# A graph attention stage: units of two groups, one pacing wait each, parts of z added in PSUM

## The chip, the cores and the metric

The kernel runs on one core of a Trainium2 chip. The metric is the device time of one execution in microseconds, and the time of a kernel is the median of its runs. The engines are called PE (matrix products), DVE (vector), ACT (activations), POOL (here it issues the gathers) and SP (here it issues plain loads and stores).

## The reference

Three graph layers with means over neighbours, a layer norm, then one attention layer on the same graph, with a residual and a layer norm. Only the attention layer is touched by the change. N is 12500 nodes, E is 200000 edges (src, dst), D is 256, with K = 4 heads of R = 16.

```python
ZU = einsum('nd,kdr->knr', Z, U)              # 4 heads of 16 numbers for each node
zs = ZU[:, src, :]
zd = ZU[:, dst, :]
logits = (zs * zd).sum(-1) / sqrt(R)
alpha = softmax of logits over the edges of each dst
agg = segment_sum(alpha[..., None] * zs, dst)
ssa = einsum('k,knr,kdr->nd', softmax(head_w), agg, U)
Z_half = 0.5 * Z + 0.5 * ssa
grad_step = Z_half + 0.5 * ((Z_half - Z_half @ Dmat.T @ Dmat) @ Dmat)
x = layernorm(x + relu(grad_step - 0.05))
```

The edges are sorted by dst, so the edges of a node lie side by side.

## The kernel before, in words

The first 5560 us are the three graph layers, with which the change has nothing to do. Then `fast_attention` (from line 1006) works on the edges in **groups** of GT = 14 tiles of 128 edges, 112 groups, the last of 9 tiles. The nodes that the edges of one group meet fit in 128 rows from a start that is known for the group; `delta` holds how far the start moves from one group to the next. A row of `zu_d` holds the 64 numbers of a node (KR = 64).

For a group the kernel does the following.

- SP loads the rows of the group's own nodes (`zn`, the 64 numbers; `zb` and `zT`, the 256 numbers and their transpose) and, spread over all partitions, the position of each edge's dst among the group's rows (`ohT` before it is a one-hot).
- POOL issues 14 indirect gathers (`gather`, line 121), one for each tile, which fetch the row of each edge's source into `zs`.
- ACT makes the one-hot `ohT` (nodes by edges) in two instructions of 1792 elements, lines 1043 and 1044. DVE makes the other one-hot `oh` (edges by nodes), line 477.
- ACT and DVE split `zn` into a rounded part and the rest, the two parts of z, lines 1048 and 1049.
- **pD** (PE, line 1055): for each tile one matmul, ohT against both parts of z side by side, gives each edge the 64 numbers of its dst twice, 128 columns. Half a group of seven tiles fills 896 columns of PSUM.
- DVE multiplies this with `zs` (`zz`, line 1063, 896 elements) and sums it to the logits (`lg`, line 1066). ACT takes the exponential (line 1069) and copies it next to pD (line 1071), DVE multiplies with `zs` (`wf`, line 1072), and ACT and DVE split the result into two parts again (`w`, lines 1075 and 1076).
- **pA** (PE, line 1083): `oh` against `w`, added over the 14 tiles, gives for each node the sums over its edges. The edges of a node can begin in the group before, so `carry` (line 486) adds the previous group's sums, shifted by `delta`.
- ACT and DVE add the two parts (`part`, line 1091; `acc`, line 1093) and divide (`den`, `ag`, lines 415 to 418). PE turns the result (**pT**, line 1097), ACT copies it (`agT`, line 425), and PE makes the gradient step (**pO**, line 402 with `zT`, line 408 with `agT`).
- ACT and DVE finish: relu (line 432), residual, layer norm (lines 355 to 360), and SP stores 128 rows.

`group(g)` is a generator of five steps: gathers up to pD and `w`; pA with the carry; `part` up to pT; `agT` and pO; the end. `order_of` calls, for each new group, first the new group, then the next step of the four groups before it. `in_order` fixes the order of the matmuls on PE as they are written.

Two gathers of a group are held back. The first one (j = 0) waits for the last pD of the group before (`shown`), and the eighth (j = H) for the pA of two groups before (`summed`). In POOL's order, twelve free gathers of a group stand ahead of these held ones.

```python
if j == 0 and g:
    hold_back(shown[-1], i)
if j == H and 1 < g < NG - 1:
    hold_back(summed[g - 2], i)
```

Of the kernel before, what the change touches and what calls it, by code (L numbers as in the profile page):

```python
# [9 lines left out]
F32 = mybir.dt.float32  # L10
# [13 lines left out]
P = 128  # L24
NB = 125
TE = 125
GT = 14
# [21 lines left out]
def tile_gnn_resnorm(  # L49
# [70 lines left out]
    def gather(dst_ap, table, idx):  # L120
        return nc.gpsimd.indirect_dma_start(  # L121
            out=dst_ap, out_offset=None, in_=table,
            in_offset=bass.IndirectOffsetOnAxis(ap=idx, axis=0))
# [10 lines left out]
    def hold_back(first, then):  # L134

        tc.add_manual_dep(then.ins, first.ins.name, DONE, reason="the pace of the gathers")
# [317 lines left out]
    def load_rows(pairs, g, first_of=None):  # L454

        rows = group_rows(g, loads[0], AFTER, first_of)
        for t, table in pairs:
            loads[0] = nc.sync.dma_start(t, rows_of(table, rows))
# [15 lines left out]
    def onehot(wk, nodes, r, dt=F32, name="oh", op=OP.is_equal, bufs=2, m=GT, behind=None):  # L474

        oh = wk.tile([P, GT, P], dt, name=name, bufs=bufs)
        i = nc.vector.tensor_tensor(oh[:, :m], r[:, :m].unsqueeze(2).to_broadcast([P, m, P]),  # L477
                                    nodes.unsqueeze(1).to_broadcast([P, m, P]), op=op)
        if behind is not None:
            after(behind, i)  # L480
        return oh

    def carry(wk, pa, d, before):
        sh = wk.tile([P, P], F32, name="sh")
        nc.vector.tensor_scalar(sh, steps, d, None, op0=OP.is_equal)
        return nc.tensor.matmul(pa, sh, before, start=False, stop=True)  # L486

    def fast_sage():
        with ExitStack() as fx:
# [516 lines left out]
    def fast_attention():  # L1006
        loads[0] = None
        H = GT // 2
        with tc.tile_pool(name="att", bufs=2) as wk, \
                tc.tile_pool(name="att_c", bufs=1, space=PSUM) as cps, \  # L1010
                tc.tile_pool(name="att_ps", bufs=1, space=PSUM) as ps:
            nodes = group_consts(cps)
            order, sums = [None], [None]
            shown, summed = [], []

            def in_order(first, last):
                if order[0] is not None:
                    after(order[0], first)
                order[0] = last

            def group(g):

                T = GT if g < NG - 1 else LT
                zb = wk.tile([P, D], F32, name="zb", bufs=8)
                zT = wk.tile([P, DC, P], F32, name="zT", bufs=6)
                zn = wk.tile([P, KR], F32, name="zn", bufs=3)
                load_rows([(zn, zu_d), (zb, z_d), (zT, zt_d)], g)

                ohT = wk.tile([P, GT, P], F32R, name="ohT", bufs=3)
                rT = ohT.bitcast(F32)[:, :T].rearrange("p j e -> p (j e)")  # L1030
                nc.sync.dma_start(rT, rel_d[g * GT:g * GT + T, :].rearrange("j e -> (j e)")[None, :]
                                  .to_broadcast([P, T * P]))
                zs = wk.tile([P, GT, KR], F32, name="zs", bufs=6)
                for j in range(T):
                    i = gather(zs[:, j], zu_d, srcI[:, g, j:j + 1])

                    if j == 0 and g:
                        hold_back(shown[-1], i)
                    if j == H and 1 < g < NG - 1:
                        hold_back(summed[g - 2], i)  # L1040
                oh = onehot(wk, nodes, rel[:, g], F32R, bufs=3, m=T)
                oT = ohT[:, :T].rearrange("p j e -> p (j e)")
                nc.scalar.activation(oT, rT, AF.Abs, bias=npidx)
                nc.scalar.activation(oT, rT, AF.Relu, scale=-1.0, bias=1.0)

                z2 = wk.tile([P, K, 2, R], F32R, name="z2", bufs=3)
                zk = zn.rearrange("p (k r) -> p k r", r=R)
                nc.scalar.activation(z2[:, :, 0], zk, AF.Copy)
                nc.vector.tensor_tensor(z2[:, :, 1], zk, z2.bitcast(F32)[:, :, 0], op=OP.subtract)

                w = wk.tile([P, GT, 2 * AW], F32R, name="w", bufs=3)
                for a, n in ((0, H), (H, T - H)):

                    pd = ps.tile([P, (H + 1) * 2 * KR], F32, name="pD", bufs=2)
                    mm = [nc.tensor.matmul(pd[:, j * 2 * KR:(j + 1) * 2 * KR], ohT[:, a + j],  # L1055
                                           z2.rearrange("p k i r -> p (k i r)"), start=True, stop=True)
                          for j in range(n)]
                    in_order(mm[0], mm[-1])
                    shown.append(mm[-1])

                    zg = zs[:, a:a + n].rearrange("p t (k r) -> p (t k) r", r=R)
                    zz = wk.tile([P, H * K, 2, R], F32, name="zz")[:, :n * K]
                    nc.vector.tensor_mul(zz, zg.unsqueeze(2).to_broadcast([P, n * K, 2, R]),  # L1063
                                         pd[:, :n * 2 * KR].rearrange("p (m i r) -> p m i r", i=2, r=R))
                    lg = wk.tile([P, H, K], F32, name="lg")[:, :n]
                    nc.vector.reduce_sum(lg.rearrange("p t k -> p (t k)"), zz.rearrange("p m i r -> p m (i r)"),  # L1066
                                         axis=AX.X)
                    wf = wk.tile([P, H, AW], F32, name="wf")[:, :n]
                    nc.scalar.activation(wf[:, :, KR:], lg, AF.Exp, scale=0.25)
                    pe = pd[:, H * 2 * KR:H * 2 * KR + n * K].rearrange("p (t k) -> p t k", k=K)  # L1070
                    nc.scalar.activation(pe, wf[:, :, KR:], AF.Copy)
                    nc.vector.tensor_mul(wf[:, :, :KR].rearrange("p t (k r) -> p t k r", r=R),  # L1072
                                         zs[:, a:a + n].rearrange("p t (k r) -> p t k r", r=R),
                                         pe.unsqueeze(3).to_broadcast([P, n, K, R]))
                    nc.scalar.activation(w[:, a:a + n, :AW], wf, AF.Copy)
                    nc.vector.tensor_tensor(w[:, a:a + n, AW:], wf, w.bitcast(F32)[:, a:a + n, :AW], op=OP.subtract)
                yield
                own = None
                if g == NG - 1:
                    own, *mm = own_gradient(ps, zT)  # L1080
                    in_order(*mm)
                pa = ps.tile([P, 2 * AW], F32, name="pA")
                mm = [nc.tensor.matmul(pa, oh[:, j], w[:, j], start=j == 0, stop=g == 0 and j == T - 1)  # L1083
                      for j in range(T)]
                if g:
                    mm.append(carry(wk, pa[:, :AW], delta[:, g:g + 1], sums[0]))
                in_order(mm[0], mm[-1])
                summed.append(mm[-1])
                yield
                part = wk.tile([P, AW], F32, name="part")  # L1090
                nc.scalar.activation(part, pa[:, AW:2 * AW], AF.Copy)
                acc = wk.tile([P, AW], F32, name="acc", bufs=3)
                nc.vector.tensor_add(acc, part, pa[:, :AW])
                sums[0] = acc
                ag = attention_mean(wk, acc, 1e-30, OP.max)
                pt = ps.tile([P, P], F32, name="pT")
                mm = nc.tensor.transpose(pt[:KR], ag, ident)  # L1097
                in_order(mm, mm)
                yield
                agT = attention_turned(wk, pt, P)  # L1100
                pg, *mm = gradient_step(ps, zT, agT, own)
                in_order(*mm)
                yield
                o, made = attention_end(wk, zb, pg)
                store_rows([(o, out)], g, made)
                yield

            live = []  # L1110
            for g in range(NG):
                live.append(group(g))
                if g < NG - 1:
                    order_of = [g, *range(max(0, g - 4), g)]
                else:
                    order_of = [g, g - 4, g - 3, g - 2, g - 1, g - 3, g - 2, g - 1, g - 2, g - 1, g - 1] + [g] * 4
                for k in order_of:
                    next(live[k])
            assert all(next(s, 0) == 0 for s in live)


# [202 lines left out]
```

## Time and profile before

| what | value |
|---|---|
| runs | 7839.01, 7910.11, 7911.72 us, median 7910.11 |
| the profiled execution | 7864.61 us, span 7862.8 us |
| attention stage, first gather starts | 5562.54 us |
| attention stage, last gather starts | 7821.82 us |
| PE, DVE, ACT, POOL busy over the span | 70%, 48%, 43%, 61% |
| PE, DVE, ACT, POOL busy, 6000 to 7500 us | 48%, 52%, 44%, 66% |
| granted TensorE clock, whole span | 0.776 |
| granted TensorE clock, 6000 to 7500 us | 0.50 |
| one group, mean of 74 groups in 6000 to 7500 us | 20.27 us |

The profiled execution is one more execution, with its own time; sums over the trace are made against that time. A line of the groups of instructions gives the source line, the engine, the operation, the tile written and those read, the shape and the count, then the busy time and the mean duration in ns, and after the second bar the idle time of the engine just before these instructions, with what ended it. "Issue" is idle time in which nothing that the profile shows was waited for. A row of the timeline gives start, duration, engine, line and what was done, and in brackets how long the engine had been idle before it and what released it. PEld is PE's weight load. The ends of matmuls are modelled. Where the released instruction waited for several things, the profile names the one that came last by its records.

### The profile page before, as it was taken

To read this page: it belongs to the slowest core of one execution; us is meant where nothing else is said; L and a number is where in the kernel's file an instruction comes from. 1 tells how busy PE (TensorE), PEld (TensorE's weight loads), DVE (VectorE), ACT (ScalarE), POOL (GpSimd) and SP (SyncE) were. 2 spreads that over 40 slices of the span, in tenths; PEclk is the share of its full clock that TensorE was granted. 3 is DMA by queue.
4 is the path that set the end of the run, shared out by engine and by line. 5 is a ranking of instruction groups with operands and counts; after the bars stand their busy time and mean duration, and the time that the engine had idled before them with its cause. 6 is when DMAs were issued, how large, how long until landed. Compare 5 with 4: busy or idle time off the path is not lost.

```text
span 7862.8 us, 85871 instructions
## 1 busy us (share of the span) xinstructions
PE 5525.1 (70%) x23570; PEld 4415.0 (56%) x23570; DVE 3772.2 (48%) x9563; ACT 3353.2 (43%) x6092; POOL 4799.9 (61%) x4977
## 2 busy tenths in 40 slices
PE   4688888888588888888588888887444444444445
PEld 3466666666466666666476676665343443344344
DVE  4555444444244444344344555554455555555555
ACT  2333333333255555444354454444344444444443
POOL 5556656556466666565565565656466666666665
PEclk6899999889799999998798999998655555555555
DMA  7777777777466766665576676665222222222222
GB/s 209 243 235 233 247 235 249 235 238 249 154 218 215 225 217 221 202 217 184 161 220 200 212 225 209 213 195 168 89 92 91 88 89 91 91 85 92 91 87 67
DMA packets 896848, 1391.60 MB, mean 177 GB/s; under 512 B 191296, under 2 KB 540504, under 8 KB 892253
## 3 DMA queue, kind: packets, MB, share of 16 engines
q1 hardware_dynamic: 654927, 834.75, 32.3%
q0 software_dynamic: 213152, 496.65, 21.6%
q10 hardware_dynamic: 28270, 54.56, 2.0%
q8 instruction: 189, 3.10, 0.2%
q14 instruction: 310, 2.54, 0.1%
HBM read 1175.15 MB, written 210.33 MB: 176 GB/s over the span
## 4 chain that ended last, share of the span: by engine, by line
PE 27%; DVE 8%; issue 6%; another core or an unknown queue 4%; POOL 3%; DMA 3%; ACT 1%; DVEq 0%; ACTq 0%; POOLq 0%
PE px L783 8%; PE pD L1055 3%; PE pA L1083 3%; POOL zs L121 3%; PE pA L908 3%; DMA zs<-zu_d,srcI 3%; PE pO L402 2%; DVE zz L1063 2%; PE pO L408 2%; DVE lg L1066 1%; PE pO L375 1%; DVE wf L1072 1%; PE pT L384 1%; PE pA L486 1%
## 5 line engine op out<-in xcount | busy, mean ns | idle before, releaser
L121 POOL DMA_INDIRECT xg<-h_d,srcI x2128 | 2079.8, 977 | 1404.0 <-issue 646.9
L783 PE MATMUL px<-c,hz 128*128 128x512 f32 x8232 | 2396.7, 431 | 224.0 <-ACT c L777 106.1
L121 POOL DMA_INDIRECT zs<-zu_d,srcI x1563 | 1496.9, 958 | 821.5 <-issue 422.0
L783 PEld LDWEIGHTS px<-c,hz 128*128 128x128 f32 x8232 | 1593.9, 202 | 580.1 <-ACT c L777 126.8
L777 ACT ACTIVATE c<-c 128x1024 fp32r<-128x1024 uint8 (+1 forms) x1274 | 1119.1, 891 | 1431.1 <-remote 469.9
L121 POOL DMA_INDIRECT xg<-in_x_dram,srcI x1218 | 1159.9, 952 | 769.1 <-PE pA L911 304.5
L477 DVE TENSOR_TENSOR oh<-rel,gconst 128x1792 fp32r<-128x1792 f32 (+1 forms) x354 | 713.8, 2017 | 1239.2 <-PE pO L408 414.6
L902 DVE TENSOR_TENSOR hl<-xg,hl 128x256 fp32r<-128x256 f32 x2128 | 777.5, 419 | 509.2 <-ACT hl L900 370.1
L1097 PE MATMUL pT<-ident,ag 128*64 128x128 f32 x112 | 47.2, 422 | 1158.9 <-DVE ag L418 760.9
L900 ACT ACTIVATE hl<-xg 128x512 fp32r<-128x512 f32 x1216 | 619.9, 568 | 292.4 <-PE pA L908 62.1
L1097 PEld LDWEIGHTS pT<-ident,ag 128*64 128x64 f32 x112 | 14.4, 128 | 1238.4 <-DVE ag L418 813.1
L911 PE MATMUL pA<-xg,oh 128*128 128x258 f32 x2520 | 659.1, 418 | 58.7 <-ACT agg L933 36.9
L908 PE MATMUL pA<-hl,oh 128*128 128x512 f32 x2128 | 604.6, 421 | 85.3 <-issue 82.8
L911 PEld LDWEIGHTS pA<-xg,oh 128*128 128x128 f32 x2520 | 528.7, 212 | 166.1 <-ACT agg L933 42.2
L673 ACT ACTIVATE win<-pc 128x392 uint16<-128x392 f32 x512 | 252.5, 496 | 662.7 <-remote 222.9
L908 PEld LDWEIGHTS pA<-hl,oh 128*128 128x128 f32 x2128 | 419.6, 200 | 195.3 <-issue 96.9
L661 DVE TENSOR_SCALAR oa<-iota,kt 128x128 bf16<-128x128 f16 x1024 | 268.9, 263 | 278.2 <-PE pA L911 108.7
L1055 PE MATMUL pD<-z,ohT 128*128 128x128 f32 x1563 | 360.9, 418 | 54.2 <-DVE lg L1066 19.1
L365 DVE TENSOR_TENSOR pO<-b,pO 128x256 f32<-128x256 f32 x306 | 130.7, 427 | 533.2 <-remote 295.4
L1055 PEld LDWEIGHTS pD<-z,ohT 128*128 128x128 f32 x1563 | 346.9, 333 | 55.1 <-issue 25.3
L1063 DVE TENSOR_TENSOR zz<-zs,pD 128x896 f32<-128x896 f32 x224 | 242.1, 1081 | 272.5 <-DMA zs<-zu_d,srcI 137.9
L1083 PE MATMUL pA<-w,oh 128*128 128x136 f32 x1563 | 361.4, 418 | 0.0
(255 smaller groups left out, 7368.2 us busy)
## 6 DMA issues: line engine op xcount, KB each, us to landing
hz<-hs_d SPq DMA_DIRECT2D x637, 512.0 KB
c<-cnt_d SPq DMA_DIRECT2D x112, 896.0 KB
ohT<-rel_d SPq DMA_DIRECT2D x111, 896.0 KB
hs_d<-hs SPq DMA_DIRECT2D x218, 256.0 KB
cnt_d<-win ACTq DMA_DIRECT2D x32, 1568.0 KB
xg<-h_d,srcI POOLq DMA_INDIRECT x2128
c<-cnt_d SPq DMA_DIRECT2D x70, 448.0 KB
zs<-zu_d,srcI POOLq DMA_INDIRECT x1563
```

The lines of the kernel that those rows point to most:

```text
L121: return nc.gpsimd.indirect_dma_start(out=dst_ap, out_offset=None, in_=table, in_offset=bass.IndirectOffsetOnAxis(ap=idx, axis=0))
L477: i = nc.vector.tensor_tensor(oh[:, :m], r[:, :m].unsqueeze(2).to_broadcast([P, m, P]), nodes.unsqueeze(1).to_broadcast([P, m, P]), op=op)
L661: nc.vector.tensor_scalar(oa[:, c], iota16[:, :P], kt[:, 0, at], None, op0=OP.is_equal)
L777: nc.scalar.activation(c32.rearrange("p (k d) -> p k d", d=P), c8[:, :, b % CB], AF.Copy)
L783: made.append(nc.tensor.matmul(px[f][i], hz[:, b % ZB, a:a + P].bitcast(F32R), c32[:, i * 512:(i + 1) * 512], start=b == 0 and part == 0, ...
L900: nc.scalar.activation(hi[:, j:j + n, :W], xg[:, a + j:a + j + n, :W], AF.Copy)
L902: nc.vector.tensor_tensor(lo[:, j, :D], xg[:, a + j, :D], hf[:, j, :D], op=OP.subtract)
L908: mm.append(nc.tensor.matmul(pa, oh[:, a + j], hl[:, j].rearrange("p i d -> p (i d)"), start=first, stop=stop))
L911: mm.append(nc.tensor.matmul(pa[:, :W], oh[:, a + j], xg[:, a + j, :W], start=first, stop=stop))
L1055: mm = [nc.tensor.matmul(pd[:, j * 2 * KR:(j + 1) * 2 * KR], ohT[:, a + j], z2.rearrange("p k i r -> p (k i r)"), start=True, stop=True) f ...
L1063: nc.vector.tensor_mul(zz, zg.unsqueeze(2).to_broadcast([P, n * K, 2, R]), pd[:, :n * 2 * KR].rearrange("p (m i r) -> p m i r", i=2, r=R))
L1083: mm = [nc.tensor.matmul(pa, oh[:, j], w[:, j], start=j == 0, stop=g == 0 and j == T - 1) for j in range(T)]
```

## The change

The attention stage now works in units of two groups: `plan` has 54 pairs of groups and four single groups at the end.

- `unit(gs)` has one step for the loads, gathers and `ohT`; one for each half group of pD (four in a pair); one for each half group of `zz` to pA (four); then `acc` to pT, pO and the end, each done once for both groups. The calls are arranged so that, on PE, the pA halves of one unit alternate with the pD halves of the next.
- Of a unit's 28 gathers one is held back, the very first, by the last pD of the unit before. The wait for pA is gone.
- pD: for each tile two matmuls of 64 columns, one for each part of z, add in PSUM. A half group takes 448 columns, with the exponentials in the same bank. There are four such banks. `zz` and `lg` read 448 elements.
- A third one-hot, `past`, places the edges of the first group among the nodes of the second. The matmuls of the first group's halves are followed by seven more each, which add these edges to the second group's sums. The carry of the second group starts from the previous unit's sums, shifted by both steps (`two`).
- `zs` has three buffers of two groups, `zb` five, `zT` four, `w` six half groups, `oh` and `past` four in all.

The core of the diff:

```diff
-            def group(g):
+            def unit(gs):
...
-                    if j == 0 and g:
-                        hold_back(shown[-1], i)
-                    if j == H and 1 < g < NG - 1:
-                        hold_back(summed[g - 2], i)
+                        if i == 0 and j == 0 and shown:
+                            hold_back(shown[-1], it)
...
-                    mm = [nc.tensor.matmul(pd[:, j * 2 * KR:(j + 1) * 2 * KR], ohT[:, a + j],
-                                           z2.rearrange("p k i r -> p (k i r)"), start=True, stop=True)
-                          for j in range(n)]
+                    mm = [nc.tensor.matmul(pd[:, j * KR:(j + 1) * KR], ohT[:, i * GT + a + j], z2[:, i, part],
+                                           start=part == 0, stop=part == 1) for j in range(m) for part in range(2)]
...
+                        oh = onehot(wk, nodes, rel[:, g], F32R, bufs=4, m=T[i])
+                        if i + 1 < n:
+                            rp = wk.tile([P, GT], F32, name="rp")
+                            nc.vector.tensor_scalar(rp, rel[:, g], delta[:, g + 1:g + 2], None, op0=OP.subtract)
+                            past = onehot(wk, nodes, rp, F32R, bufs=4)
...
+                    mm = [nc.tensor.matmul(pa[:, i], oh[:, a + j], w[:, j], start=a + j == 0 and i == 0,
+                                           stop=ends and j == m - 1) for j in range(m)]
+                    if i + 1 < n:
+                        mm += [nc.tensor.matmul(pa[:, i + 1], past[:, a + j], w[:, j], start=False, stop=False)
+                               for j in range(m)]
+                    if g0 and a + m == T[i]:
+                        mm.append(carry(wk, pa[:, i, :AW], delta[:, g:g + 1] if i == 0 else two[:, g:g + 1], sums[0],
+                                    i == n - 1))
...
+            PAIRS = NG // 2 - 2
+            plan = [[2 * k, 2 * k + 1] for k in range(PAIRS)] + [[g] for g in range(2 * PAIRS, NG)]
...
+            for k, gs in enumerate(plan):
+                live.append(unit(gs))
+                go(k)
+                for i in range(4, 1, -1):
+                    go(k - i)
+                for h in range(4):
+                    if k and h < 2 * len(plan[k - 1]):
+                        go(k - 1)
+                    if h < 2 * len(gs):
+                        go(k)
```

## The prediction

> **What bounds the kernel now.** Only the attention stage changes, so I first looked where it lies. In the page's 40 slices the clock falls to half and POOL rises in the last twelve (first line below); the stage's first gather starts at 5562.54 us, its last ends at 7822.8, and 40 us follow. That is 2260 of the 7862.8 us of span, for 112 groups. Then the busy time by stretch:
>
> ```profile
> PEclk6899999889799999998798999998655555555555
> ```
>
> ```profile
> core 0: us, PE busy (x) PEld busy (x) DVE busy (x) ACT busy (x) POOL busy (x), PEclk, DMA share, GB/s
> 6000.00:6500.00 500.00, 235.14 (x900) 197.20 (x900) 264.06 (x498) 220.66 (x372) 330.25 (x345) 0.50 0.30 90
> ```
>
> No engine is full. POOL leads with 330 of 500, and it issues the gathers. The groups of instructions in 6000 to 7500 (74 groups, 20.27 us each) show how:
>
> ```profile
> L121 POOL DMA_INDIRECT zs<-zu_d,srcI x1036 | 993.6, 959 | 506.5 <-issue 281.7 <-PE pO L408 171.2 <-remote 35.6
> L1055 PEld LDWEIGHTS pD<-z,ohT 128*128 128x128 f32 x1036 | 229.9, 333 | 0.0
> L1063 DVE TENSOR_TENSOR zz<-zs,pD 128x896 f32<-128x896 f32 x148 | 160.5, 1084 | 156.8 <-DMA zs<-zu_d,srcI 100.2 <-remote 47.8 <-PE pO L408 4.4
> L477 DVE TENSOR_TENSOR oh<-rel,gconst 128x1792 fp32r<-128x1792 f32 x74 | 149.6, 2022 | 446.8 <-PE pO L408 297.5 <-PE pO L402 68.0 <-PE pD L1055 44.4
> L1069 ACT ACT_TABLE_LOAD x74 | 94.9, 1283 | 1.3
> L1097 PEld LDWEIGHTS pT<-ident,ag 128*64 128x64 f32 x74 | 9.5, 128 | 837.8 <-DVE ag L418 549.3 <-DVE w L1076 193.8 <-issue 57.6
> ```
>
> A gather costs 0.95 us busy and 0.30 us "issue", 1.25 us. Fourteen are 17.5 us; the other 2.8 us of a group are one pause. In the timeline of POOL a pause is the row with the long idle time:
>
> ```profile
> 5652.16 0.95 POOL L121 DMA_INDIRECT zs<-zu_d,srcI  x1 [0.30 <-issue]
> 5656.85 0.95 POOL L121 DMA_INDIRECT zs<-zu_d,srcI  x1 [3.75 <-remote]
> ...
> 6525.33 0.95 POOL L121 DMA_INDIRECT zs<-zu_d,srcI  x1 [0.30 <-issue]
> 6529.21 0.95 POOL L121 DMA_INDIRECT zs<-zu_d,srcI  x1 [2.93 <-PE pO L408]
> ```
>
> The second ends a run of 14 gathers, the first a run of 27 without a stop. Over the stage 88 runs of 14 end in a pause of 2.83 us at the median. The wait is for pD (and pA); the timeline of all engines around 6529 shows that PE has nearly always done that earlier, and that its posts arrive late and together:
>
> ```profile
> 6518.71 0.42 PE L1097 MATMUL pT<-ident,ag 128*64 128x128 f32 x1 [10.91 <-DVE w L1076]
> 6518.72 3.11 PEld L1083 LDWEIGHTS pA<-w,oh 128*128 128x128 f32 x14
> ...
> 6522.20 3.23 PE L1055 MATMUL pD<-z,ohT 128*128 128x128 f32 x14
> ...
> 6527.17 1.22 PE L408 MATMUL pO<-gu,agT 64*128 64x256 f32 x2
> 6528.93 2.02 DVE L477 TENSOR_TENSOR oh<-rel,gconst 128x1792 fp32r<-128x1792 f32 x1 [6.93 <-PE pO L408]
> 6528.98 0.23 ACT L1091 ACTIVATE part<-pA 128x68 f32<-128x68 f32 x1 [5.88 <-PE pO L408]
> ```
>
> DVE's oh waits for pA, done at 6522.0; ACT's part for the carry, done at 6522.5; the gather at 6529.21 for pD, done at 6525.4. All three start within 0.3 us, 3.8 to 7 us late and only once gathers have stopped. So a group costs 14 gathers plus one stop in which PE's posts come through. PE then idles 11 us for DVE's ag.
>
> **The change part by part**, for a pair (two groups, 40.54 us now).
>
> *One pacing wait a unit* (hold_back on shown[-1], gather j=0 alone). POOL still issues 28 gathers, 35.0 us, plus 0.3 us for the slow gather or two of each group (the surplus over 0.95 in the rows). Two pauses of 2.83, less the 0.30 that each gather has anyway, go: −5.06. One comes, after 28 gathers. Its length is not shown; from below it is the 2.83 of a run of 14, from above twice that, 5.66, if the pause grows with the gathers behind it. The run of 27 is the nearest row, 3.75, so +3.45. Pair: 38.7 us, −1.6 to −1.8. On POOL the 27 free gathers of a unit stand ahead of the held one, and behind it those of the next unit. SP issues as many loads as before, in pairs.
>
> *Parts of z added in PSUM.* Each tile now has two 64-column pD matmuls, each with a weight load: 56 loads a pair for 28. Fourteen loads take 3.11 us in a burst, 0.22 each, so +6.2 us on PE; from below 0, if equal weights were free, from above 28 × 0.333 = 9.3. I take the burst's spacing. zz and lg halve to 448 elements (wf with 448 takes 616 ns against zz's 1084): 4 × (0.47 + 0.52) = −3.9 us on DVE.
>
> *First group's edges also meet the second's nodes.* Fourteen more pA matmuls, +3.1 us on PE, one more one-hot of 2.02 and rp at 0.2 on DVE. They remove the second group's wait for the first's sum; its carry uses `two` and the previous pair's sum.
>
> *Merged acc, den, o, agT and g* save about 1.2 us of DVE. Two of four table loads go: 2 × 1.28 on ACT. DVE is 2.9 us less a pair, ACT some 4. Both lie beside gathers.
>
> *Buffers* (zs three pairs, zT 4, zb 5, w 6 halves): the next pair's first gather waits for wf of three pairs back, over 35 us earlier. Nothing. The wait of zz for its own gathers (100.2 us above) goes too, since a pair is used one unit after it was fetched.
>
> **What is late next.** The loop left runs: last pD posts, DVE works from zz to ag, PE does pT, four pA halves and four pD halves, last pD. On DVE, in program order from the first zz to ag: three one-hots 6.1, four zz 2.4, three lg 1.7, two wf 1.2, two w 1.3, two g 0.8, the small ones 1.9, together 15.4; rows that follow each other overlap by some 0.07, 22 of them 1.5: 14 us. PE has 42 pA, 56 pD, two carries of two loads: 102 × 0.22 = 22.4. With 0.9 for pT and posts: 37.3 us, 1.4 under the 38.7 of POOL. That is all the cover: PE's +9.3 us cost nothing only because the loop, even if nothing overlaps, is shorter than 28 gathers and a pause. Were the sum 1.4 us too low, each further microsecond would cost 54.
>
> **Two rules against rows.** The Trainium skill, TensorE: Matmul & The Clock Gate, in its part on the clock gate, says a TensorE busy for about 3.4 us is let up to full clock. By it the 22.4 us of a pair would shrink to some 13 and the loop to 28. The row says 0.50 in a stretch full of bursts of 8 us; I keep 22.4.
> The same page, section "The cost: per-tile semaphore tail", lets the post of a burst come about 25 + 4.7 per tile + 26.3 ns per post after it: 0.12 us for 14 tiles with one post. Then the gather at 6526.6 would hardly have stopped, and after the change there would be no pause: 35.3 us a pair. The rows have 3.8 to 7 us. I take the rows; the rule is my fast rival.
>
> **The sum.** There are 54 pairs (and four single groups as before): 54 pauses fewer, 54 × −2.53 = −137 us; 54 pauses longer, 54 × 0.92 = +50. Sum −87 us, about −1.1%. The fill at the start and the 40 us after the last gather I leave as they are, ±10 us. The profiled execution took 7864.6 us (span 7862.8); it becomes 7777. The runs' median is 7910.1, 45 us higher, the same program spreading over 0.9% (7839 to 7912). On the median: **7822 us**. About 1% is what a measurement of this kernel can tell from no change.
>
> **The rivals.**
> - *Slower: a held post stalls PE inside the long run.* On ACT, o (waits for pO) and agT (waits for pT) stand ahead of w of the second group's halves, and PE's third pA half waits for w. pT ends some 14.5 us after the pause; if its post reaches ACT at t, the last pD is at t + 2 (agT, w) + 43 × 0.22 + 0.9, t + 12.3. It decides from t = 26.4, a lateness of 12 us. Held to the pause (t about 38.4) a pair takes 50.7, +10.2 × 54 = +550 us; midway, t = 32.4, 44.7, +225, so **8135 us**. For it: posts were 7 us late in runs of 14, one of pD 8.6 us late in the long runs at the start (pD's end 5577.65, zz at 5586.31), and the runs are now twice as long. SP's zT load, waiting for pO ahead of zn and ohT, can be caught in the same way. Against it: pT follows an idle PE, and its post to ACT was prompt in every group looked at.
> - *No change:* a pause in proportion to its run (5.66), or DVE's 14 or PE's 22.4 short by 3 us: 40 to 41.5 us a pair, **7895 us**.
> - *Fast:* posts come in time, no pause: 54 × −5.06 = −275, **7635 us**. For it: with 28 gathers between waits PE has its work done sooner relative to POOL if DVE can start early on posts that trickle through. Against it: the loop of 37.3 us is longer than 35.3 unless DVE and PE overlap by 2 us, and every long run here ended in a pause.
> - *The change doesn't do what it says*, a second stop in each unit: it would need a buffer wait on POOL, and none is near. I give it nothing.
>
> **How the numbers follow.** Forecast 0.41 (7800 to 7850), slower rival 0.34, no change 0.13, fast 0.12. The forecast's gain lies barely over 1%, so of its 0.41 about 0.31 counts as faster, 0.08 as no change, 0.02 as slower; with the fast case faster 0.43, same 0.20 (most of the no-change case), slower 0.37. The range 7620 to 8150 holds the fast case's centre and the nearer half of the slow one, leaving out about 0.2.
>
> **What would show it.** Right: in the timeline of POOL, runs of 28 gathers 1.25 us apart, one pause of 3.3 to 4 us, 38.4 to 39 us a pair; PE busy about 28 us a pair at clock 0.50; zz near 0.6 us. Wrong: a waits row of PE's pA for w or ACT's agT for pT of several microseconds (slower rival), or a pause above 5 us with PE still at work when gathers stop (loop too long); no pause at all (fast).

## The result, and the profile after

The changed kernel takes 8342.29 us at the median of six runs (8303.95 to 8386.72), the kernel before 7908.53 us at the median of six. The ratio is 1.0569, interval 1.0528 to 1.0609: 434 us slower. The forecast was 7822 us, 87 us less than the kernel before. The profiled execution of the changed kernel took 8386.72 us (span 8384.9).

One thing must be known to read the runs further down. A *post* is the signal by which an engine tells another that a piece of work is done. In some of the jobs (sets of runs made together) the kernel before took 6425 to 6433 us at the median instead of 7825 to 7910. The jobs ran on several chips, and one chip showed both. In the kernels traced in the faster jobs, PE's posts came 0.01 us after their matmuls, and POOL made hardly any stops; the kernel before itself was not traced there. I call these conditions *prompt* and those of the two profiles *late*. Most of the difference lies ahead of the attention stage: its first gather starts at 4417 us in e1 (prompt) and at 5563 us in the profile before. Times are compared only with the kernel before in the same job.

In the page of the changed kernel the granted clock of the attention stage is what it was:

```profile
PEclk6799999998898988987989998975555555555555
```

The busy time by stretch shows POOL less busy, not more. PE is busier, DVE and ACT less:

```profile
core 0: us, PE busy (x) PEld busy (x) DVE busy (x) ACT busy (x) POOL busy (x), PEclk, DMA share, GB/s
6000.00:6500.00 500.00, 295.74 (x1172) 267.34 (x1172) 188.26 (x372) 144.94 (x233) 272.43 (x285) 0.50 0.27 74
```

The groups of instructions in 6000 to 7500 hold what the prediction asked for: POOL's idle time before a gather, the weight loads of pD, zz, the one-hots, the table loads and pT.

```profile
L121 POOL DMA_INDIRECT zs<-zu_d,srcI x860 | 826.8, 961 | 673.9 <-PE pD L1055 405.4 <-issue 257.8 <-DMA zs<-zu_d,srcI 7.9
L1055 PEld LDWEIGHTS pD<-z,ohT 128*128 128x128 f32 x1702 | 404.4, 323 | 521.7 <-issue 521.7
L477 DVE TENSOR_TENSOR oh<-rel,gconst 128x1792 fp32r<-128x1792 f32 x61 | 122.8, 2013 | 0.0
L1073 DVE TENSOR_TENSOR zz<-zs,pD 128x448 f32<-128x448 f32 x121 | 73.0, 603 | 814.0 <-PE pD L1055 539.6 <-remote 270.5 <-DMA zs<-zu_d,srcI 4.0
L1078 ACT ACT_TABLE_LOAD x31 | 39.8, 1283 | 0.5
L1114 PEld LDWEIGHTS pT<-ident,ag 128*64 128x64 f32 x62 | 5.6, 140 | 20.2 <-issue 20.2
```

The gather still costs 0.96 + 0.30 us. What is new is the second line: the weight loads of pD had no idle time before them, and now 521.7 us of "issue", time in which PE waits for nothing that the profile shows. POOL's timeline has one stop a unit, and it is 14 us long (14.1 at the median of the stage) where 3.75 was forecast:

```profile
6527.86 0.94 POOL L121 DMA_INDIRECT zs<-zu_d,srcI  x1 [0.30 <-issue]
6542.87 0.94 POOL L121 DMA_INDIRECT zs<-zu_d,srcI  x1 [14.07 <-PE pD L1055]
```

The stop before that one ended at 6493.67, so a unit takes 49.2 us, of which 28 gathers are 35.1. The timeline of the other engines between the two stops shows what PE does:

```profile
6499.71 0.42 PE L1114 MATMUL pT<-ident,ag 128*64 128x128 f32 x1
...
6502.81 3.13 PE L1055 MATMUL pD<-z,ohT 128*128 128x64 f32 x14
...
6508.67 0.55 PEld L486 LDWEIGHTS pA<-acc,sh 128*128 128x128 f32 x2
6509.47 0.29 PEld L1055 LDWEIGHTS pD<-z,ohT 128*128 128x128 f32 x1 [0.25 <-issue]
6510.18 0.21 PE L1055 MATMUL pD<-z,ohT 128*128 128x64 f32 x1 [0.77 <-issue]
6510.89 0.29 PEld L1055 LDWEIGHTS pD<-z,ohT 128*128 128x128 f32 x1 [1.14 <-issue]
...
6531.32 0.21 PE L1055 MATMUL pD<-z,ohT 128*128 128x64 f32 x1 [0.49 <-issue]
6532.04 0.62 DVE L1073 TENSOR_TENSOR zz<-zs,pD 128x448 f32<-128x448 f32 x1 [27.77 <-PE pD L1055]
...
6539.43 3.17 PE L1055 MATMUL pD<-z,ohT 128*128 128x64 f32 x14
```

Read it from the top. From 6499.71 PE runs at full pace: 14 pD matmuls in 3.1 us. At 6509.47, 15.8 us and some 115 recorded PE instructions after the gathers resumed, it falls to one start every 0.7 us, for 24 us and some 34 instructions. I call this the **crawl**. It ends at 6533.4, 5.6 us after the last gather of the run started, and the rest goes at full pace again. The first pD half ended at 6505.94, and zz, which waits for it, starts at 6532.04: its post is 26.1 us late. Every one of the 30 units in 6000 to 7500 us has its crawl; in 27 of them it starts 14 to 16 us after the gathers resumed, in three only after 18 to 20.

So the loop of a unit is: zz to ag on DVE 14.0 us (6532.04 to 6546.01), ag to pT 2.7 (PE has the pO of an earlier unit first), pT to the end of the first pD half 6.2, its post 26.1 late. That is 49.0 us of the 49.2. Seen from POOL, the stop of 14.07 us is 4.6 from the end of the last gather (6528.80) to the end of the crawl, then 9.2 in which PE does what was left up to the last pD half (6542.60), then 0.3 to the next gather.

### The profile page after: what moved, and what is told of

Same layout as the page of the kernel before. It is cut to its first block, busy times and chain, and to the rows that moved or that the text cites. A ratio compares the mean times of both kernels' runs of the same rounds, so it can differ in the third digit from the quotient of the medians.

```text
span 8384.9 us, 89710 instructions
## 1 busy us (share of the span) xinstructions
PE 6070.8 (72%) x25887; PEld 4985.2 (59%) x25887; DVE 3615.1 (43%) x9347; ACT 3171.7 (38%) x5716; POOL 4799.0 (57%) x4977
## 4 chain that ended last, share of the span: by engine, by line
PE 41%; issue 16%; another core or an unknown queue 6%; DVE 3%; ACT 2%; DMA 1%; POOL 0%; SPq 0%; ACTq 0%; DVEq 0%; POOLq 0%
PE px L783 12%; PE pD L1055 8%; PE pA L908 4%; PE pA L1090 4%; PE pO L1122 3%; PE pO L375 2%; PE pA L1093 2%; PE pO L1124 2%; DVE hl L902 1%; PE pT L384 1%; PE pA L486 1%; ACT hl L900 1%; ACT c L777 1%; PE pO L742 1%
## 5 line engine op out<-in xcount | busy, mean ns | idle before, releaser
L1055 PE MATMUL pD<-z,ohT 128*128 128x64 f32 x3126 | 716.7, 365 | 979.8 <-issue 961.4
L1055 PEld LDWEIGHTS pD<-z,ohT 128*128 128x128 f32 x3126 | 739.5, 323 | 924.6 <-issue 923.8
L1073 DVE TENSOR_TENSOR zz<-zs,pD 128x448 f32<-128x448 f32 x224 | 135.2, 603 | 1483.2 <-PE pD L1055 910.0
L911 PE MATMUL pA<-xg,oh 128*128 128x258 f32 x2520 | 659.3, 418 | 51.3 <-ACT agg L933 35.3
L1078 ACT ACTIVATE wf<-lg 128x28 f32<-128x28 f32 x224 | 50.0, 223 | 1347.5 <-DVE lg L1075 1319.3
L1090 PE MATMUL pA<-w,oh 128*128 128x136 f32 x1563 | 396.3, 416 | 140.3 <-issue 135.9
L1090 PEld LDWEIGHTS pA<-w,oh 128*128 128x128 f32 x1563 | 364.8, 329 | 176.3 <-issue 169.0
```

The costliest lines, as they stand in the source:

```text
L911: mm.append(nc.tensor.matmul(pa[:, :W], oh[:, a + j], xg[:, a + j, :W], start=first, stop=stop))
L1055: mm = [nc.tensor.matmul(pd[:, j * KR:(j + 1) * KR], ohT[:, i * GT + a + j], z2[:, i, part], start=part == 0, stop=part == 1) for j in ran ...
L1090: mm = [nc.tensor.matmul(pa[:, i], oh[:, a + j], w[:, j], start=a + j == 0 and i == 0, stop=ends and j == m - 1) for j in range(m)]
```

## The experiments

**First job: pacing alone, a second wait, fewer PE instructions, no gathers.** Theory A, drawn from the two traces, is that a long unbroken run of gathers delays PE's posts and then PE. Theory B is that the extra PE work does the harm. Theory C is that PE's own supply of instructions is at fault.

e1 changes the pacing alone, in the kernel before:

```diff
-                    if j == 0 and g:
+                    if j == 0 and g and g % 2 == 0:
                         hold_back(shown[-1], i)
-                    if j == H and 1 < g < NG - 1:
-                        hold_back(summed[g - 2], i)
```

> The kernel before with its pacing alone changed: one gather of every 28 waits for pD, the wait for pA is gone. PE's instructions are those of the kernel before (some 78 a group). Theory A: while gathers follow each other without a stop, PE's completions come through only for about the first 10 us; after that they drain slowly, posts are late, and once some 60 are pending PE itself crawls at about 0.7 us an instruction until the gathers end. Then the second group of each run cannot start before the stop: 52 to 60 us for two groups in place of 40.5, some 8550 to 8950 us in all. Theory B: the run of 28 is harmless, and the changed kernel is slow because of its own extra PE work: two groups take about 39 us, some 7800 us in all.

e2 gives the changed kernel a second wait, and keeps the gathers in the order of the groups. Of this edit and those of e5 and e7 below only the core is shown, and the comments in them are added here:

```diff
+                if n > 1:
+                    fetch(1, 0, GT, summed[-1] if summed else None)   # group 2; summed: last pA half
```

> The changed kernel with a second stop: the first gather of the unit's second group waits for the first pA half of the unit before, and gathers go in the order of the groups, so no run is longer than 14. Theory A: PE's crawl starts about 112 instructions after the second stop in place of the first, so it begins later and is shorter: 43 to 46 us a unit in place of 49.2, some 8030 to 8200 us. Theory B (PE's own work bounds it): no change from 8340, or slower by the second stop, 2 to 3 us a unit, up to 8500.

e3 leaves out the second part of z:

```diff
-    start=part == 0, stop=part == 1) for j in range(m) for part in range(2)]
+    start=True, stop=True) for j in range(m) for part in range(1)]
```

> The changed kernel with the second part of z left out of pD: 28 matmuls and 28 weight loads of a unit are gone, and the logits miss that part. Theory A: after the resumption PE gets through 146 instructions (112 fast and 34 crawling) before the gathers have ended, whatever they are; 80 are left in the changed kernel, 24 here, so a unit takes 49.2 - 56 x 0.11 = 43 us: some 8010 us. Theory B (each PE instruction slow in itself, 49.2 us for some 226): 12 us less a unit, some 7700 us.

e5 loads consecutive rows from SP instead of gathering:

```diff
-                        it = gather(zs[:, i * GT + j], zu_d, srcI[:, g, j:j + 1])
+                    it = nc.sync.dma_start(zs[:, i * GT:i * GT + T[i]],
+                                           zu_d[row:row + P * T[i], :].rearrange("(p j) c -> p j c", j=T[i]))
```

> The changed kernel with the gathers of the attention stage replaced by one plain load of a group's 1792 rows from SP's queue, consecutive rows in place of the edges' sources; POOL then issues nothing in that stage. Theory A (POOL's gathers hold PE's completions): no crawl at 0.7 us, posts prompt, a unit at PE's and DVE's own pace, 28 to 37 us: 7250 to 7720 us. Theory C (the crawl has to do with PE's own instruction supply, not with gathers): the crawl stays where it is, about 112 instructions after each of PE's idle times, a unit stays above 45 us, above 8100 us.

This job fell into prompt conditions. The kernel before took 6432.57 us, e1 6426.33 (ratio 0.9994, 0.9984 to 1.0004), e2 6431.62 (0.9995), e3 6428.98 (0.9994), and e5 6030.62 (0.9373, 0.9346 to 0.9400). No theory had expected that three kernels with different pacing and different PE work would tie with the kernel before. The timeline of POOL in e1 says why: rows 1.25 us apart, with no stop at all between one set of 28 and the next.

```profile
5500.22 0.95 POOL L121 DMA_INDIRECT zs<-zu_d,srcI  x1 [0.30 <-issue]
5501.47 0.94 POOL L121 DMA_INDIRECT zs<-zu_d,srcI  x1 [0.30 <-issue]
```

The 1563 gathers take 1973 us (4417 to 6390), 1.26 us each. Where posts are prompt the stage is bound by POOL's gathers alone, and neither pacing nor PE's work counts. What tells the theories apart has to be run in late conditions.

**The changed kernel again**, to see which conditions go with which result.

> The changed kernel itself, unaltered. In the runs that shared a chip with e1 to e5 the kernel before took 6432 us, with gathers 1.25 us apart and PE's posts 0.01 us after their matmuls, where the first profile had stops of 2.8 us and posts up to 7 us late. Theory D: late posts and PE's crawl belong to the conditions of the first runs, not to the kernels; where posts are prompt both kernels are held by POOL's 1563 gathers of 1.25 us and the change is worth nothing, 6390 to 6440 us beside 6432. Where posts are late again (the kernel before near 7900), the changed kernel is near 8340 again. Theory E: the extra PE work costs by itself: 1 to 3% slower also where posts are prompt.

Late conditions: the kernel before 7825.23 us, the changed one 8257.90, ratio 1.0558 (1.0473 to 1.0643). The crawl starts again some 15 us after the gathers resumed in 23 of the 31 units in 6000 to 7500 us; in the other 8 it starts after 19 to 23. The loss is there again; theory E's part, a loss in prompt conditions, was not tried with this kernel itself, only with e2 and e3, which have its units and tie.

**Pacing alone and no gathers, in late conditions.**

> The kernel of e1 again: the kernel before with its pacing alone changed, one gather of every 28 held back. If the kernel before takes some 6430 us here, posts are prompt and this tells nothing new (6430 again). If it takes some 7850: theory A (a long run of gathers delays PE's posts and then PE itself) gives 52 to 60 us for two groups, 8500 to 8900 us; theory B (the extra PE work of the changed kernel does the harm, not its pacing) gives about 39 us, 7700 to 7800 us.

e1b took 8353.56 us beside 7907.23: ratio 1.0583 (1.0478 to 1.0688), 446 us. That is the whole loss of the changed kernel, with none of its extra PE work. Theory B falls. The price forecast for theory A was too high: two groups take 49.7 us, not 52 to 60, and the kernel 8354 us, not 8500 to 8900. The timeline of e1b shows the same stop on POOL:

```profile
6531.55 0.94 POOL L121 DMA_INDIRECT zs<-zu_d,srcI  x1 [0.31 <-issue]
6547.25 0.94 POOL L121 DMA_INDIRECT zs<-zu_d,srcI  x1 [14.75 <-PE pD L1053]
```

and, on the other engines, how it comes about. Here PE has too few instructions in a run to crawl. The posts are late by themselves:

```profile
6511.62 1.22 PE L408 MATMUL pO<-gu,agT 64*128 64x256 f32 x2
...
6525.22 1.09 DVE L1061 TENSOR_TENSOR zz<-zs,pD 128x896 f32<-128x896 f32 x1 [9.77 <-DMA zs<-zu_d,srcI]
...
6537.35 0.47 ACT L432 ACTIVATE g<-pO,shrink 128x256 f32<-128x256 f32 x1 [10.34 <-remote]
...
6537.95 1.15 DVE L1070 TENSOR_TENSOR wf<-zs,pD 128x448 f32<-128x448 f32 x2 [10.38 <-ACT pD L1069]
...
6540.25 0.13 PEld L1095 LDWEIGHTS pT<-ident,ag 128*64 128x64 f32 x1 [28.13 <-DVE ag L418]
```

The zz at 6525.22 waited for its own gathers, but that wait is not the one that ends last. pO ended at 6512.84. ACT's g, which waits for it, starts at 6537.35, 24.5 us later. Behind g in ACT's queue stands the copy of the exponentials to pD, behind that DVE's wf, w and ag, and behind ag PE's pT, idle for 28 us. Only when the gathers had ended did the second group of the run begin.

> The kernel of e5 again: the changed kernel with the attention stage's gathers replaced by one plain load of consecutive rows a group, from SP's queue. Where posts are prompt: 6030 us again. Where the kernel before takes some 7850: theory A (POOL's gathers delay the posts) gives no crawl in this stage and a unit of some 30 us as in e5, 7150 to 7400 us; theory C (PE's own instruction supply) leaves the crawl at 0.7 us an instruction and a unit above 45 us, above 8000 us.

e5b took 7177.73 us in the same job, ratio 0.9093 (0.9001 to 0.9185). No crawl is left in the attention stage, and PE has no idle time in the stretch shown:

```profile
6100.00:6600.00 500.00, 500.00 (x2043) 446.04 (x2042) 330.04 (x636) 255.28 (x405) 0.00 (x0) 0.50 0.38 129
```

A unit takes 27.9 us here, with all the PE work of the change; in prompt conditions (e5) it takes 28.0. So without gathers in this stage the two conditions do not differ in it. Theory C, that PE's supply of instructions fails by itself, falls: without the gathers PE is not held up. Whether the gathers slow PE by way of that supply is left open.

**A second wait, a third, and plain loads from POOL**, all in one job in late conditions (the kernel before 7827.08 us).

> The changed kernel with a second stop for POOL's gathers: the second group's first gather waits for the first pA half of the unit before; no run is longer than 14. e1b showed that the long run alone costs 446 us. Theory A (length of the run, then PE's crawl after some 112 instructions): the crawl begins after the second stop only, is shorter, and a unit takes 43 to 46 us in place of 49.2: 8050 to 8200 us beside some 7900 for the kernel before. Theory B2 (what matters is one wait in place of two, wherever it is): back at the kernel before, 7850 to 7950.

e2b missed both forecasts: 8216.30 us, 1.0506 (1.0411 to 1.0602), a unit of 48.5 us. The trace tells why. The pA half that the second group waits for is posted before POOL gets there: 14 gathers after the stop at 6528.93 are done at 6546.4, and the next gather starts at 6546.90. The wait is there, the stop is not, and the run is as long as before.

e7 places two waits in PE's busy stretch:

```diff
+                    fetch(1, 0, H, summed[-1] if summed else None)    # gathers 15 to 21: last pA half
                 for i, a, m in halves:
+                    if n > 1 and len(pds) == 2:
+                        fetch(1, H, GT, shown[-1])                    # gathers 22 to 28: own second pD half
```

> The changed kernel with three stops a unit, runs of 14, 7 and 7: the second group's first gather waits for the first pA half of the unit before, its eighth for the unit's own second pD half, so that the stops fall into PE's busy stretch. Theory A: after the third stop fewer than 112 PE instructions are left, no crawl at 0.7 us; a unit takes 35.0 us of gathers and three stops of 1.3 to 2.8 us, 40 to 43 us: 7850 to 8030 us, all of the loss or nearly all won back with all the extra PE work still there. Theory B (the extra PE work costs by itself): above 8200.

e7 took 7847.99 us (18 runs): 1.0036 (1.0016 to 1.0057). Of three waits, two became stops, as the timeline of POOL shows:

```profile
6511.80 0.95 POOL L121 DMA_INDIRECT zs<-zu_d,srcI  x1 [2.53 <-remote]
...
6541.87 0.95 POOL L121 DMA_INDIRECT zs<-zu_d,srcI  x1 [3.73 <-remote]
...
6551.98 1.42 POOL L121 DMA_INDIRECT zs<-zu_d,srcI  x1 [1.66 <-remote]
```

One run of 21, one of 7, and a unit of 40.2 us from 6511.80 to 6551.98. The loss shrinks from 5.7% to 0.4%, with every other part of the change still in place (28 gathers take 40.8 us at the mean of 6000 to 7500, where the kernel before took 40.5). PE still crawls in the run of 21, in the unit shown for some 14 us; it costs no more because the rest of PE's work is done in the short run. e2b and e7 both keep the gathers in order, and differ only in where the waits stand.

> The changed kernel with POOL's gathers replaced by plain loads of 128 consecutive rows, still issued one by one from POOL and held back in the same way. Without any of them (e5b) PE was busy all the time and a unit took about 28 us. Theory A1 (whatever POOL issues in a long row delays PE's posts): the crawl stays, a unit takes 45 to 50 us, 8100 to 8400 us. Theory A2 (the indirect gathers alone do it): no crawl, a unit is bounded by the 28 loads or by PE, 28 to 37 us, 7180 to 7700 us.

e4 took 7104.23 us, 0.9084 (0.9018 to 0.9150). POOL issued 28 plain loads a unit at 0.54 us each, and PE was busy throughout:

```profile
6500.00:7000.00 500.00, 500.00 (x2042) 446.05 (x2043) 330.14 (x634) 251.56 (x407) 259.07 (x490) 0.50 0.40 127
```

No post is late: in one unit a pD half ends at 6522.77, and its zz starts at 6522.81. Theory A1 falls, and A2 fits, with a time just under its 7180 to 7700. But the plain loads leave POOL more stops than the gathers did, as its timeline shows:

```profile
6510.52 4.21 POOL L1041 DMA_DIRECT2D zs<-zu_d  x8 [11.23 <-PE pD L1056]
6515.54 6.31 POOL L1041 DMA_DIRECT2D zs<-zu_d  x12 [0.81 <-DMA zs<-zu_d]
6523.81 4.32 POOL L1041 DMA_DIRECT2D zs<-zu_d  x8 [1.96 <-issue]
```

In 6000 to 7000 us the longest row of loads without a stop over 1 us lasts 17 us, as long as the 14 gathers after which the kernel before had posts 3.8 to 7 us late. A row of plain loads as long and as close as 28 gathers was not run, so that it would be harmless is not shown.

**Fewer PE instructions in the same long run.**

> The changed kernel with the second part of z left out of pD (the logits miss it): 56 PE instructions of a unit's 226 or so are gone, the single wait of 28 gathers stays. e1b showed that the long run alone is enough for the whole loss. Theory A (PE gets through about 146 instructions before the gathers have landed, whatever they are, then does the rest at 0.11 us each): a unit takes 43 us in place of 49.2, some 8000 us where the kernel before takes 7900. Theory F (a unit of a long run takes some 49 us whatever PE's count of instructions, since the posts are held to the end of the run in any case, as in e1b with 156 of them): no better than 8250. Where the kernel before takes 6430: 6430 again, and nothing new.

e3b took 8106.31 us beside 7829.54: 1.0342 (1.0264 to 1.0420), between the two forecasts. A unit takes 46.0 us. The crawl starts again after 115 to 118 recorded instructions, 15.5 us into the run, so its start is set by neither pD's form nor the place in the program. Whether the count of instructions or the time sets it is not settled: here both are the same as before. But the saving is 3.2 us a unit, not 6: the posts are released at the end of the run in any case, and DVE's work after them remains. Both A and F are part of it.

**A stop that has nothing to do with PE.** e8 is e1b with one more stop, and with the gathers kept in the order of the groups; the first gather of every second group waits for the landing of the gather before it:

```diff
+                    if last[0] is not None:
+                        after(last[0], i)
                     if j == 0 and g and g % 2 == 0:
                         hold_back(shown[-1], i)
+                    if j == 0 and g % 2:
+                        hold_back(last[0], i)
+                    last[0] = i
```

> The kernel of e1b (the kernel before, one wait for pD in 28 gathers) with one more stop that has nothing to do with PE: the first gather of every second group waits until the gather before it has landed; gathers go in the order of the groups. Theory A (PE's posts get through whenever the gathers pause, whatever for): the posts of the first group's burst come in that pause of some 3 to 4 us, and the two groups are back at 40.5 to 42 us: 7850 to 7980 us where the kernel before takes some 7850. Theory G (the wait for PE itself is what keeps the pace, a short pause for a landing lets nothing through): as e1b, 8300 to 8400 us. Where the kernel before takes 6430: some 6600 to 6650, by 56 pauses of 3 to 4 us.

Its first three runs (e8, e8b, e8c) fell into prompt conditions: ratios 1.0176, 1.0168 and 1.0154. There 56 stops cost 98 to 110 us, 1.8 to 2.0 us each; the first expectation had 3 to 4. The fourth fell into late ones.

> The kernel of e8 a last time. If the kernel before takes some 7850 here: theory A (PE's posts get through whenever the gathers pause, whatever for) gives 40.5 to 42 us for two groups, 7850 to 7980 us; theory G (only a wait for PE itself keeps the pace) gives 8300 to 8400 us, as e1b. If it takes some 6430: 6535 again.

7850.18 us beside 7837.84, ratio 1.0012 (0.9989 to 1.0035). The stop for the landing is 2.14 us, and the wait for pD after it is back at 3 us:

```profile
6530.96 0.95 POOL L121 DMA_INDIRECT zs<-zu_d,srcI  x1 [2.14 <-issue]
6551.52 0.94 POOL L121 DMA_INDIRECT zs<-zu_d,srcI  x1 [3.06 <-remote]
```

As the landing stop ends, the held posts come through:

```profile
6531.16 0.26 ACT L1052 ACTIVATE z<-zn 128x64 fp32r<-128x64 f32 x1 [9.64 <-remote]
6531.16 1.09 DVE L1067 TENSOR_TENSOR zz<-zs,pD 128x896 f32<-128x896 f32 x1 [2.75 <-remote]
6532.86 0.46 ACT L432 ACTIVATE g<-pO,shrink 128x256 f32<-128x256 f32 x1
```

pO ended at 6526.62, and g starts 6.2 us later where e1b had 24.5. With a stop of 2 us that waits for nothing of PE, the 446 us of e1b are won back. What the old pacing bought was the stop, not the order between PE and POOL. Theory G falls. One rival is not run apart: the order of the gathers, which e1b does not have. Against it speaks e2b, which has that order, lacks the second stop and lost 5.1%.

## Why the prediction was wrong

- **What bounds the kernel** was read rightly: POOL's gathers and one stop a group, in which PE's posts come through. The runs of e7 and e8d, where stops came back and the loss went, show that this reading is the cause and not only a picture.
- **The step that failed is the length of the one pause.** The sum took 3.75 us, from one row after a run of 27, with 5.66 as the upper end. It measured 14.07: the fault is +10.3 us a unit, times 54 units 557 us, where the forecast missed by 520 in all. The row came from the fill of the pipeline. The upper end scaled the stop with the gathers behind it, though the trace of before held a stop of 7.33 us after a run of 40 gathers (at 5619.60) and the working itself had posts 8.6 us late; a held post stalls everything that waits behind it, and that has no such scale. What stood behind the pause was the loop: it was priced at 37.3 us, with 0.9 for pT and posts together, and it measured 49.0, because one post came 26.1 us late.
- **PE's 102 loads at 0.22 us, 22.4 us.** From pT to the end of the last pD half it is 42.9 us (6499.71 to 6542.60). The 20.5 us more are the crawl. Its instructions, at full pace, do cost what was said: in 6000 to 7500 us PE is busy 28.9 us for each 28 gathers where 19.3 were before, +9.6 against +9.3 forecast.
- **DVE's 14 us from zz to ag** measured 14.0. zz took 603 ns for the 0.6 forecast. DVE fell by 2.9 us a unit (21.14 to 18.26; 2.9 forecast), ACT by 3.4 (17.8 to 14.4; some 4). None of it showed in the time, as said; and e7, with all of this and stops restored, is within 0.4% of the kernel before.
- **The cover** of 1.4 us between loop and gathers was the point to distrust. It was called all the cover there is, and yet the loop in it had posts that come at once, while the pause was priced from rows in which posts come only when the gathers stop. The two do not go together.
- **The slower rival** had the kind right and the place wrong. Held posts in a run twice as long stalled PE, at 225 to 550 us; 434 came, and its upper case of 50.7 us a pair lies 1.5 from the 49.2 measured. But pT's post, named as the held one, was prompt (agT starts 0.06 us after pT's end in the unit shown). The held one was the first pD half's, and PE itself slowed down, which the rival did not have. At 0.34 it had too small a share: the trace of before already had the late posts of runs of 14.
- **Rules against rows.** Taking the rows was right both times: the clock stayed 0.50, and posts were up to 26 us late. The 0.12 us was an estimate carried over from another case: the Trainium skill, TensorE: Matmul & The Clock Gate, section "The cost: per-tile semaphore tail", gives its rule for small matmuls packed side by side into one array, not for 14 whole ones in a row. In prompt conditions posts come 0.01 us after their matmuls, and the fast rival's 35.3 us a pair is what POOL then takes (e1). There the kernel before took the same time as e1, e2 and e3, so pacing has nothing left to give.
- **No second stop in each unit**, given nothing: right.

Open: what in the chip holds PE's completions back while indirect gathers follow each other, why PE gets through some 115 instructions before it crawls, and what makes conditions late or prompt. The runs show each of these and explain none, and the 60 pending posts that theory A took for the start of the crawl were seen in no run. Every timed run has a span and a clock read from the profiler's records, so whether the recording itself takes part is not known either.

## What to carry to other kernels

A wait that looks like pure pacing can be doing work: before taking it away, find out what the other engines get done in the stop, and check that a wait put elsewhere still stops anything (e2b's second wait was satisfied early and made no stop). When one resource holds back completions, price the new run from the work that queues behind the held completion, in order, on each engine, and not by scaling the old stop. If a stage's time hangs on such a thing, test it first with a stop that waits for something harmless, as e8d did.

## What the runs showed of the hardware that was not expected

- In late conditions a run of indirect gathers from POOL, 1.25 us apart, holds PE's posts back by up to 26 us, and after some 115 PE instructions since its start PE goes on at one instruction in 0.7 us until about 5.6 us after the last gather. 28 plain loads a unit from POOL, with stops of some 1 to 2 us between their rows and one of 11, do nothing of the kind (e4).
- Stops after every 14 gathers are enough to let the posts through, also where such a stop is 2.1 us long and waits for a landing (e8d).
- The same kernel took 6425 to 6433 us in some jobs and 7825 to 7910 in others, with the same program.
- PE busy for 1497.9 of 1500 us (5600 to 7100 in e5b) was still granted a clock of 0.50 in this stage.
